# The last unit of a four-layer graph network: two passes over half the query tiles each, against one pass over ten tiles and two late ones over three

## The chip, the core and the metric

The kernel runs on one core of a Trainium2 chip. A core has a matrix engine (TensorE, PE in the profile; PEld is its loading of weights, the stationary operand), a vector engine (VectorE, DVE), an engine for activation functions (ScalarE, ACT), a general one (GpSimd, POOL) and SyncE (SP), which issues transfers. They run side by side and wait for one another by semaphores; 16 DMA engines move data. On chip there is SBUF, where operands lie in 128 partitions, and PSUM, where matmuls accumulate, in eight banks of 512 float32 columns. The metric is the device time of one execution, in microseconds (us); several executions are made and their median counts.

## The reference, cut to what matters

Four layers act on 3327 nodes with 512 features; each ends in `x = layernorm(x + layer(x))`. Layers 0, 2 and 3 are graph attention, layer 1 averages neighbours. The change lies in layer 3, which has 4 heads of 128 features:

```python
h = (x @ W).reshape(N, 4, 128).transpose(1, 0, 2)
si, sj = einsum('hnd,d->hn', h, a1), einsum('hnd,d->hn', h, a2)
e = si[:, :, None] + sj[:, None, :]
e = where(e > 0, e, 0.2 * e)
e = where(adj[None] > 0, e, -9e15)
attn = softmax(e, axis=-1)
out = elu(einsum('hij,hjd->hid', attn, h))
x = layernorm(x + out)
```

## The kernel before, in words

The nodes are 26 tiles of 128 (`NT`); a half of the query nodes is 13 tiles, 1664 columns (`HALF`, `IW`). Layer 3 runs as eight units: for each half of the queries, one unit per head (`s` = 0 to 3). A unit (`unit`, line 429) goes over the 26 key tiles `j`. For each tile, `weights` makes with one VectorE instruction (L420) the unnormalized weights `t` in float32, keys in partitions and queries in columns: a maximum of a row of query terms (`rb`) with a key's term, times the 0/1 mask. ScalarE makes from `t` a step function `y` in 8 bits (L425), from which the softmax denominators come. TensorE multiplies the values of the key tile (`vj`, 128 features as stationary operand, loaded from the DRAM tensor `vd` by SyncE, two tiles at a time) with `t` and accumulates into four PSUM banks `po`, cut as `CUTS` says: 448, 448, 384 and 384 columns (L482). Every four tiles `den` adds up the denominators in the banks `pd` (L446). A product of float32 operands runs as two passes on TensorE, each with its own weight load.

There are three buffers for `t` (pool `at_t`), seven for `y`, three for `vj`. Jobs of the unit before are handed on in a list (`background`) and one is run after each tile; a second list (`aside`) holds other work. So while unit (1, 2) is over and unit (1, 3) runs, its results are transposed (L519), divided by the denominators, put through ELU and added to the residual `g` (`final`, L1472 to L1477), after its denominators went through DRAM and came back as `pes` (L571, L583, L593), and 13 statistics of the first 384 features are taken (L1436). The first two tiles' weights of the next unit are made at the end of a unit (`start`). The order on TensorE is the order of the program; the other engines' instructions are ordered by a planner, except where `tc.keep_in_program_order` pins them among themselves.

The last unit (`last_unit`, line 639) differs. Its 13 query tiles are done in two passes (`e`) over all 26 key tiles: the first over 896 columns (`WA`, 7 query tiles), the second over 768 (`WB`, 6 query tiles). Each pass makes its own weights and steps (L420, L425 with widths 896 and 768), loads the values anew (L677), multiplies them in two banks (L681), and adds denominators in `pd` and in two spare banks (L664), which are copied and summed in the end (L670, L701, L737). The 7 tiles of the first pass are finished while the second pass runs, by jobs (`last_jobs` and `slots`): transposes (L729), reciprocals (L741 to L743), division (L1506), exponential, addition, statistics, the inverse square root on POOL (`rsqrt`, L152 and L153), factors (L1482), scaling by VectorE or ScalarE (L1490, L1488), and a store per tile, issued in turn by SyncE and POOL (L133). The 6 tiles of the second pass are finished after it, in the tail.

Of the kernel before, what the change touches and what calls it, by code (L numbers as in the profile page):

```python
# [1 line left out]

# [5 lines left out]
F32 = mybir.dt.float32  # L8
# [10 lines left out]
P = 128  # L19
# [13 lines left out]
def kernel(  # L33
# [24 lines left out]
    assert WA // 2 <= 512  # L58
    PIECES = (0, 48, 72, 32)
# [40 lines left out]
    c1a = const.tile([P, 2, 4], F32, name="c1a")  # L100
# [5 lines left out]
    nc.vector.tensor_reduce(c1a, c1.rearrange("p o (k s) -> p o s k", s=4), AX.X, ALU.add)  # L106
# [133 lines left out]
    class Layer:  # L240
# [177 lines left out]
        def weights(self, tp, yp, j, h, rb, i0, lo=0, w=IW, pinned=False):  # L418
            t = tp.tile([P, IW], F32, name="t")
            ins = nc.vector.scalar_tensor_tensor(t[:, :w], rb[:, lo:lo + w], self.qc[:, j, h:h + 1],  # L420
                                                 mask_at[0](j, i0 + lo, w), op0=ALU.max, op1=ALU.mult)
            if pinned:
                tc.keep_in_program_order(ins)
            y = yp.tile([P, IW], F8, name="y")
            nc.scalar.activation(y[:, :w], t[:, :w], AF.Sigmoid, bias=self.bi[:, j, h:h + 1],  # L425
                                 scale=self.sc[:, j, h:h + 1], saturate=False)
            return t, y

        def unit(self, pools, half, s, background, aside, final=None, ending=None, following=None):
# [65 lines left out]
            def start(j):  # L495
                if following:
                    self.started[j] = self.weights(tp, yp, j, following[1], self.first_rows[0], following[0] * IW, 0,
                                                   WA if following == (1, NS - 1) else IW, True)
# [140 lines left out]
        def last_unit(self, pools, background, aside, slots):  # L639
            tp, yp, vp, rp, sp, po_p = pools  # L640
            s = NS - 1
            rb = self.first_rows[0]
            started, self.started = self.started, {}
            po = [po_p.tile([P, 512], F32, name=f"po{c}") for c in range(4)]
            pd, seen = self.pd, self.seen
            ob = sp.tile([P, IW], F32, name="ob", bufs=1)
            o = PIECES[s] - 8 * s
            db = sp.tile([P, WA], F32, name="db", bufs=1)
            SPARE = NT // 4 * 4 - 4
            for e, (lo, w) in enumerate(((0, WA), (WA, WB))):  # L650
                wc, nq = w // 2, w // P

                x0 = 64 * (1 - e)
                spare = po[2 - 2 * e:4 - 2 * e]

                def den(j0, ys):
                    for c in range(2):
                        for j, y in enumerate(ys):
                            if j < 2 or len(ys) == 2:
                                a, kk = pd[c], 2 * e + j % 2  # L660
                                assert (kk, c) in seen
                            else:
                                a, kk = spare[c], 2 * (1 - e) + j % 2
                            nc.tensor.matmul(a[32 * kk:32 * kk + 32, :wc], self.sden[:, j0 + j, o:o + 32],  # L664
                                             y[:, c * wc:(c + 1) * wc], start=a is not pd[c] and j0 == 0,
                                             stop=j0 + j >= NT - 2 if a is pd[c] else j0 == SPARE - 4,
                                             skip_group_check=True)
                    if j0 == SPARE - 4:
                        for c in range(2):
                            (nc.scalar.copy if c else nc.vector.tensor_copy)(  # L670
                                db[x0:x0 + 64, c * wc:(c + 1) * wc], spare[c][x0:x0 + 64, :wc])

                late = []
                for j in range(NT):
                    if j % 2 == 0:
                        vj = vp.tile([P, 2, P], F32, name="vj")
                        nc.sync.dma_start(out=vj, in_=self.vd[j * P:(j + 2) * P, s * P:(s + 1) * P]  # L677
                                          .rearrange("(t p) f -> p t f", p=P))
                    t, y = started.pop(j) if not e and j in started else self.weights(tp, yp, j, s, rb, IW, lo, w)
                    for c in range(2):  # L680
                        nc.tensor.matmul(po[2 * e + c][:, :wc], vj[:, j % 2, :], t[:, c * wc:(c + 1) * wc],  # L681
                                         start=j == 0, stop=j == NT - 1)
                    late.append(y)
                    if j % 4 == 0 and j > 0:
                        ys, late = late[:4], late[4:]
                        if j <= SPARE:
                            den(j - 4, ys)
                        else:
                            den(j - 4, ys[:2])
                            den(j - 2, ys[2:])  # L690
                    if background:
                        background.pop(0)()
                    if aside:
                        aside.pop(0)()
                den(NT - 2, late)

                for c in range(2):
                    (nc.scalar.copy if c or not e else nc.vector.tensor_copy)(
                        ob[:, lo + c * wc:lo + (c + 1) * wc], po[2 * e + c][:, :wc])
                for c in range(2):  # L700
                    (nc.scalar.copy if c else nc.vector.tensor_copy)(  # L701
                        db[64 * e:64 * e + 64, c * wc:(c + 1) * wc], pd[c][64 * e:64 * e + 64, :wc])
                jobs = self.last_jobs(e, ob, db, po[2 * e], slots)
                if e == 0:
                    while background:
                        background.pop(0)()
                    while aside:
                        aside.pop(0)()
                    background.extend(jobs)
            return jobs  # L710

        def last_jobs(self, e, ob, db, pe, slots):
            s = NS - 1
            nq = (WB if e else WA) // P
            r_, rc = (a[:, HALF + e * NA:HALF + e * NA + nq, s] for a in (rec, self.rc))
            held = []
            quads = [(q, min(4, e * NA + nq - q)) for q in range(e * NA, e * NA + nq, 4)]  # L720
            takes = []

            def transposed(k):
                if k >= len(quads):
                    return
                q0, n = quads[k]
# [3 lines left out]
                takes.append(slots(q0, n, pt, e))  # L730

            def sums():
# [3 lines left out]
                for q in range(nq):  # L736
                    nc.tensor.matmul(a[:, q, :, :], db[:, q * P:(q + 1) * P], c1a, start=True, stop=True)  # L737
# [998 lines left out]
```

## Time and profile before

| What | us |
|---|---|
| Median of three runs (3217.54 to 3222.51) | 3221.54 |
| Profiled execution, its own time | 3213.32 |
| Its span, first to last instruction | 3211.6 |
| Last unit's first product (L681) starts | 3098.9 |
| First pass's last product group ends, second pass begins | about 3149.5 |
| Last matmul group of denominators starts (L664) | 3190.99 |

The busy times that the prediction shows are sums over instructions in a stretch; an engine that is less busy than the stretch is long was waiting. A timeline row gives start, length, engine, source line, operation, output and inputs, shape, and how many instructions were merged (x4); in brackets the idle time before and what ended it. Starts of equal instructions in a row give their pitch, which is shorter than their length where they overlap. Transfers queued by SyncE stand as SPq.

### The profile page before, as it was taken

The numbers are of one execution on the slowest core, as the hardware profiler recorded it, in microseconds if no ns is written. First come the engines' busy times: TensorE is split into PE (matmuls) and PEld (weight loads), VectorE is DVE, ScalarE is ACT, GpSimd is POOL, SyncE is SP. The second block draws the span as 40 slices with busy tenths as digits, with TensorE's granted clock in tenths as the row PEclk, the third lists the DMA queues.
The fourth block names the chain that finished last, engine by engine and source line by source line (L and its number), as shares of the span: only waits on it lengthen the run. The fifth ranks groups of instructions, "written<-read, shape, count | busy, mean of one in ns | idle before, by whom it ended". The sixth has DMA issues, their size and how long they took to land. (4 is left out here: it accounts for less than half of the span.)

```text
span 3211.6 us, 45012 instructions
## 1 busy us (share of the span) xinstructions
PE 3130.1 (97%) x17934; PEld 1597.4 (50%) x17934; DVE 2611.3 (81%) x2236; ACT 2185.5 (68%) x1759; POOL 308.2 (10%) x500
## 2 busy tenths in 40 slices
PE   8899999999999999999999999999999999999997
PEld 7644343333334467777744333333337655555544
DVE  6799999999986655555489999999999666678887
ACT  2398888899882222232288989899896655568886
POOL 3100000000011122222220000000002000011211
PEclk9999999999999999999999999999999999999998
DMA  9651114111124345556341111111027311123212
GB/s 386 249 168 62 42 52 143 54 43 42 27 84 141 100 124 138 132 138 162 102 141 53 42 36 26 36 42 42 25 84 245 117 42 44 43 54 97 88 43 69
DMA packets 359920, 301.79 MB, mean 94 GB/s; under 512 B 232692, under 2 KB 291902, under 8 KB 358175
## 3 DMA queue, kind: packets, MB, share of 16 engines
q1 hardware_dynamic: 331743, 199.06, 21.1%
q0 software_dynamic: 24656, 96.63, 9.7%
q10 hardware_dynamic: 3312, 3.23, 0.4%
q8 instruction: 142, 2.33, 0.3%
q14 instruction: 67, 0.55, 0.1%
HBM read 221.97 MB, written 76.84 MB: 93 GB/s over the span
## 5 line engine op out<-in xcount | busy, mean ns | idle before, releaser
L846 ACT ACTIVATE y<-t,bi,sc 128x3328 fp8e4<-128x3328 f32 (+1 forms) x520 | 1336.1, 2604 | 97.1 <-PE pd L823 49.3
L867 PE MATMUL po<-t,vj 128*64 128x448 f32 (+1 forms) x6656 | 1269.7, 522 | 12.0 <-DVE t L845 9.4
L867 PEld LDWEIGHTS po<-t,vj 128*64 128x64 f32 x6656 | 458.1, 137 | 686.1 <-issue 625.7
L482 PE MATMUL po<-t,vj 128*128 128x448 f32 (+1 forms) x1456 | 522.6, 516 | 0.6 <-DVE t L420 0.6
L420 DVE SCALAR_TENSOR_TENSOR t<-rba,qc,mk 128x1664 f32<-128x1664 f32 (+2 forms) x234 | 408.5, 1753 | 125.3 <-PE po L482 88.0
L425 ACT ACTIVATE y<-t,bi,sc 128x1664 fp8e4<-128x1664 f32 (+2 forms) x234 | 375.4, 1618 | 189.8 <-DVE t L420 181.8
L482 PEld LDWEIGHTS po<-t,vj 128*128 128x128 f32 x1456 | 272.1, 190 | 235.2 <-issue 148.5
L845 DVE SCALAR_TENSOR_TENSOR t<-rbb,qc,mask 128x3328 f32<-128x3328 f32 (+1 forms) x130 | 380.0, 2985 | 8.4 <-PE po L867 5.4
L845 DVE SCALAR_TENSOR_TENSOR t<-rba,qc,mask 128x3328 f32<-128x3328 f32 (+1 forms) x130 | 380.7, 2982 | 7.0 <-PE po L867 6.2
L845 DVE SCALAR_TENSOR_TENSOR t<-rbb,qc,mk 128x3328 f32<-128x3328 f32 (+1 forms) x130 | 379.3, 2982 | 7.1 <-PE po L867 5.0
L845 DVE SCALAR_TENSOR_TENSOR t<-rba,qc,mk 128x3328 f32<-128x3328 f32 (+1 forms) x130 | 379.7, 2985 | 5.8 <-PE po L867 3.5
L1307 PE MATMUL acc<-zs,kt 128*128 128x512 f32 x1352 | 360.2, 420 | 0.0
L285 PE MATMUL pw<-wsb,xT 128*128 128x264 f32 (+1 forms) x1248 | 297.6, 393 | 14.3 <-DVE vt L295 8.0
L1165 ACT CAST pk<-cy 128x512 f32<-128x512 bf16 x169 | 99.7, 590 | 286.7 <-DVE kt L1179 280.1
L1307 PEld LDWEIGHTS acc<-zs,kt 128*128 128x128 f32 x1352 | 255.6, 189 | 52.1 <-PE pk L1158 0.8
L823 PE MATMUL pd<-y,sden 128*32 128x384 fp8e4 (+1 forms) x3328 | 270.1, 343 | 0.0
L285 PEld LDWEIGHTS pw<-wsb,xT 128*128 128x128 f32 x1248 | 238.5, 194 | 56.5 <-issue 9.8
L1179 DVE SCALAR_TENSOR_TENSOR kt<-pk,mb 128x512 fp32r<-128x512 f32 x169 | 116.0, 687 | 106.7 <-PE pk L1176 106.5
L823 PEld LDWEIGHTS <-sden 128*32 128x32 bf16 x3328 | 88.9, 95 | 165.0 <-issue 149.5
L295 DVE TENSOR_TENSOR vt<-pw,dc 128x256 f32<-128x256 f32 x130 | 49.9, 417 | 79.4 <-ACT dc L286 77.2
L1205 PE MATMUL pz<-wn,xT 128*128 128x512 f32 x208 | 96.9, 610 | 5.4 <-DMA wn<-in_wnT_dram 3.5
L289 ACT COPY rc<-pw 128x8 f32<-128x8 f32 (+1 forms) x78 | 12.8, 164 | 122.1 <-PE pw L285 122.1
(246 smaller groups left out, 2210.6 us busy)
## 6 DMA issues: line engine op xcount, KB each, us to landing
raw<-in_adjT_dram SPq DMA_DIRECT2D x75, 416.0 KB
vj<-v SPq DMA_DIRECT2D x169, 128.0 KB
cy<-ctd POOLq DMA_DIRECT2D x78, 256.0 KB, 4.4
h<-hd SPq DMA_DIRECT2D x61, 256.0 KB
v<-vt SPq DMA_DIRECT2D x50, 256.0 KB
md<-mask SPq DMA_DIRECT2D x26, 416.0 KB
mb<-md SPq DMA_DIRECT2D x169, 64.0 KB
mk<-md SPq DMA_DIRECT2D x50, 208.0 KB
```

The source lines that it names most:

```text
L285: nc.tensor.matmul(pw[e][:, :FW + H], xT[:, c, :], wsb[:, c, e, :], start=c == 0, stop=c == FC - 1)
L420: ins = nc.vector.scalar_tensor_tensor(t[:, :w], rb[:, lo:lo + w], self.qc[:, j, h:h + 1], mask_at[0](j, i0 + lo, w), op0=ALU.max, op1=ALU ...
L425: nc.scalar.activation(y[:, :w], t[:, :w], AF.Sigmoid, bias=self.bi[:, j, h:h + 1], scale=self.sc[:, j, h:h + 1], saturate=False)
L482: nc.tensor.matmul(po[c][k * D:(k + 1) * D, :z - a_], vj[:, j % 2, k * D:(k + 1) * D], ts[k][:, a_:z], start=j == 0, stop=j == NT - 1)
L823: nc.tensor.matmul(pd[c][32 * kk:32 * kk + 32, :w_], lhsT, rhs, start=(kk, c) not in seen, stop=last and j == NT - 1)
L845: nc.vector.scalar_tensor_tensor(to, ro, self.qc[:, j, h:h + 1], m, op0=ALU.max, op1=ALU.mult)
L846: nc.scalar.activation(yo, to, AF.Sigmoid, bias=self.bi[:, j, h:h + 1], scale=self.sc[:, j, h:h + 1], saturate=False)
L867: nc.tensor.matmul(po[c][k * D:(k + 1) * D, :z - a_], vj[:, j % 2, x_:x_ + D], t[:, k, a_:z], start=j == 0, stop=j == NT - 1)
L1165: nc.scalar.copy(pks[k % 2], carry[b, t // 4 * 4][:, t % 4:t % 4 + 2, :])
L1179: nc.vector.scalar_tensor_tensor(kt, pk, NEIGHBOURS, mb[:, t:t + 2, :], op0=ALU.is_le, op1=ALU.mult)
L1205: nc.tensor.matmul(pz, xT[:, c, :], wn[:, c, :], start=c == 0, stop=c == FC - 1)
L1307: nc.tensor.matmul(acc, kts[b, t][:, s * P:(s + 1) * P], zs(t, c), start=t == 0 and c == 0, stop=t == NT - 1 and c == 1)
```

## The change

The weights of a key tile are now made for all 1664 columns in one pass, by two instructions on VectorE and two on ScalarE: 1280 columns (ten query tiles, `KEPT`) into the buffer `t`, and 384 columns (three query tiles) into the first bytes of the key tile's own mask, whose first half is of no more use (`kept`). The pass multiplies only the first three cuts, 1280 columns, into three banks, and adds all denominators into `pd`. Afterwards the three remaining query tiles are multiplied from the kept weights: a pass over two tiles (256 columns, bank `po[3]`) and one over the last (128 columns, bank `po[0]`). Their values are loaded ahead: four tiles into `vj` buffers, the others by two transfers into two `t` buffers. While these late passes run, the ten tiles are finished by jobs set between the products (quads A, B, C of 4, 4 and 2 tiles; D is the two tiles of the first late pass, E the last tile), with the order on VectorE and ScalarE pinned. Stores are all issued by SyncE. One exponential on a single column stands ahead of the others (`warm`). `start` makes the two first tiles with the new widths. The finishing loop that stood after `L3.attention` is gone.

```diff
+    KEPT = CUTS[3][0]
...
-        def weights(self, tp, yp, j, h, rb, i0, lo=0, w=IW, pinned=False):
+        def weights(self, tp, yp, j, h, rb, i0, pinned=False, cuts=((0, IW, None),)):
...
+            for lo, hi, kept in cuts:
+                o = t[:, lo:hi] if kept is None else kept
+                ins = nc.vector.scalar_tensor_tensor(o, rb[:, lo:hi], self.qc[:, j, h:h + 1],
+                                                     mask_at[0](j, i0 + lo, hi - lo), op0=ALU.max, op1=ALU.mult)
...
+                nc.scalar.activation(y[:, lo:hi], o, AF.Sigmoid, bias=self.bi[:, j, h:h + 1],
+                                     scale=self.sc[:, j, h:h + 1], saturate=False)
...
+        def kept(self, j):
+            return mask_tiles.tiles[j][:, :4 * (IW - KEPT)].bitcast(F32)
+
+        def last_weights(self, tp, yp, j, rb, pinned=False):
+            return self.weights(tp, yp, j, NS - 1, rb, IW, pinned, ((0, KEPT, None), (KEPT, IW, self.kept(j))))
...
-            for e, (lo, w) in enumerate(((0, WA), (WA, WB))):
...
+            def den(j0, ys):
+                for c in range(2):
+                    for j, y in enumerate(ys):
+                        for e, (a_, w_) in enumerate(((c * (WA // 2), WA // 2), (WA + c * (WB // 2), WB // 2))):
+                            kk = 2 * e + j
+                            nc.tensor.matmul(pd[c][32 * kk:32 * kk + 32, :w_], self.sden[:, j0 + j, o:o + 32],
+                                             y[:, a_:a_ + w_], start=False, stop=j0 == NT - 2, skip_group_check=True)
...
+            for j in range(NT):
+                if j % 2 == 0:
+                    vj = values(j)
+                t, y = started.pop(j) if j in started else self.last_weights(tp, yp, j, rb)
+                for c, (a_, z) in enumerate(CUTS[:3]):
+                    nc.tensor.matmul(po[c][:, :z - a_], vj[:, j % 2, :], t[:, a_:z], start=j == 0, stop=j == NT - 1)
...
+            for e, (lo, w) in enumerate(((0, WA // 2), (0, WB // 2))):
                 for c in range(2):
+                    keep((nc.vector.tensor_copy, nc.scalar.copy)[c](
+                        db[64 * e:64 * e + 64, c * w:(c + 1) * w], pd[c][64 * e:64 * e + 64, :w]))
+            for c, (a_, z) in enumerate(CUTS[:3]):
+                keep((nc.vector.tensor_copy if c == 1 else nc.scalar.copy)(ob[:, a_:z], po[c][:, :z - a_]))
...
+            f = slots(transposed)
+            near = {j: values(j) for j in range(0, 4, 2)}
+            far = []
+            for lo in (4, 4 + HALF):
+                n = min(HALF, NT - lo)
+                v = tp.tile([P, IW], F32, name="t").rearrange("p (t f) -> p t f", f=P)
+                nc.sync.dma_start(out=v[:, :n, :], in_=self.vd[lo * P:(lo + n) * P, s * P:(s + 1) * P]
+                                  .rearrange("(t p) f -> p t f", p=P))
...
+            def product(acc, j, lo, hi):
+                nc.tensor.matmul(acc[:, :hi - lo], near[j // 2 * 2][:, j % 2, :] if j < 4 else far[j - 4],
+                                 self.kept(j)[:, lo - KEPT:hi - KEPT], start=j == 0, stop=j == NT - 1)
...
+            jobs = [nothing] * 3 + [
+                lambda: sums(*A, qp.tile([P, 512], F32, name="pl", tag="q")), lambda: [reciprocals(*A), f.turn(*A)],
+                lambda: [f.divide(*A), sums(*RB, po[1])], lambda: sums(*RC, po[2]),
+                lambda: [reciprocals(*RB), reciprocals(*RC)], nothing, lambda: f.turn(*B), lambda: f.divide(*B), lambda: f.turn(*C),
+                lambda: f.divide(*C), lambda: [f.add(*A), f.stats(*A)], lambda: f.add(*B), lambda: f.factors(*A), lambda: f.stats(*B),
+                lambda: f.ones(*A), lambda: f.add(*C)]
+            for j in range(NT):
+                product(po[3], j, KEPT, cut)
+                if jobs:
+                    jobs.pop(0)()
...
+            out_of(po[3], KEPT, cut)
+            jobs = [nothing] * 5 + [lambda: f.stats(*C), lambda: f.factors(*B), nothing, nothing, lambda: f.turn(*D), lambda: f.divide(*D),
+                                    lambda: [f.ones(*B), f.factors(*C), f.add(*D), f.stats(*D), f.ones(*C, (8, 9))]]
+            for j in range(NT):
+                product(po[0], j, cut, IW)
+                if jobs:
+                    jobs.pop(0)()
...
+            out_of(po[0], cut, IW)
+            f.turn(*E)
+            f.divide(*E)
+            f.factors(*D)
+            f.ones(*D)
+            f.add(*E)
+            f.stats(*E)
+            f.factors(*E)
+            f.ones(*E, (HALF - 1,))
...
+                    def divide(q0, n):
...
+                        keep(nc.vector.tensor_tensor(h[q0][:, :n], pts[q0][:, :n],
+                                                     rec[:, HALF + q0:HALF + q0 + n, NS - 1:NS]
+                                                     .to_broadcast([P, n, P]), op=ALU.mult))
+                        ex[q0] = fp.tile([P, 4, P], F32, name="e", tag="xr" if third_ else "e")
+                        keep(nc.scalar.activation(ex[q0][:, :n], h[q0][:, :n], AF.Exp))
...
+                    def stats(q0, n):
+                        for q in range(q0, q0 + n):
+                            keep(nc.vector.bn_stats(out=st[:, q, 1, :], in_=g[:, q, FB:]))
+                            keep(nc.vector.bn_aggr(out=mv[:, q, :], in_=st[:, q, :, :]))
+                        rsqrt(rs[:, q0:q0 + n, 0], mv[:, q0:q0 + n, 1])
...
+                    def ones(q0, n, by_dve=()):
+                        for q in range(q0, q0 + n):
+                            y = g[:, q, :]
+                            if q in by_dve:
+                                keep(nc.vector.tensor_scalar(y, y, rs[:, q, 0:1], rs[:, q, 1:2], op0=ALU.mult, op1=ALU.add))
+                            else:
+                                keep(nc.scalar.activation(y, y, AF.Identity, bias=rs[:, q, 1:2], scale=rs[:, q, 0:1]))
+                            store_tile(out, y, HALF + q, nc.sync)
...
+                    keep(nc.scalar.activation(warm, valid, AF.Exp))
```

## The prediction

> **What bounds the kernel now.** First the page: TensorE (PE) is busy nearly everywhere, so time is gained only where it waits or where it has stopped. The last unit starts at 3098.9 us, so next come the busy times by stage: two passes, then the tail.
>
> ```profile
> PE 3130.1 (97%) x17934; PEld 1597.4 (50%) x17934; DVE 2611.3 (81%) x2236; ACT 2185.5 (68%) x1759; POOL 308.2 (10%) x500
> ...
> 3098.90:3150.00 51.10, 46.98 (x174) 21.31 (x171) 45.03 (x63) 38.14 (x40) 9.24 (x16) 1.00 0.16 39
> 3150.00:3191.10 41.10, 40.55 (x175) 21.94 (x176) 32.38 (x56) 29.97 (x34) 4.24 (x5) 1.00 0.25 81
> 3191.10:3211.60 20.50, 2.44 (x22) 2.03 (x19) 8.60 (x27) 5.39 (x8) 4.30 (x7) 0.60 0.22 77
> ```
>
> Columns are length, busy PE, PEld, DVE, ACT, POOL, granted clock. VectorE (DVE) is nearly as full as PE in the first pass; in the tail PE is idle. The timelines give pitches:
>
> ```profile
> 3097.04 1.14 DVE L420 SCALAR_TENSOR_TENSOR t<-rba,qc,mk 128x896 f32<-128x896 f32 x1
> 3104.16 4.34 DVE L420 SCALAR_TENSOR_TENSOR t<-rba,qc,mk 128x896 f32<-128x896 f32 x4
> 3144.86 3.03 DVE L420 SCALAR_TENSOR_TENSOR t<-rba,qc,mk 128x896 f32<-128x896 f32 x3
> ...
> 3140.97 0.19 PEld L681 LDWEIGHTS po<-t,vj 128*128 128x128 f32 x1 [0.19 <-issue]
> 3141.35 0.19 PEld L681 LDWEIGHTS po<-t,vj 128*128 128x128 f32 x1 [0.19 <-issue]
> ...
> 3192.03 1.42 PEld L737 LDWEIGHTS po<-c1a,db 128*128 128x128 f32 x12
> ```
>
> A 448-column matmul pass repeats every 0.3755 us (two passes per fp32 product). The last weights of the first pass are made by 3145.95. The tail, from PE's last product to the stores:
>
> ```profile
> 3190.99 0.50 PE L664 MATMUL pd<-y,sden 128*32 128x384 fp8e4 x4
> ...
> 3200.68 2.22 ACT L1488 ACTIVATE g<-g,rs 128x512 f32<-128x512 f32 x3 [4.81 <-DVE rs L1482]
> ...
> 3202.02 0.61 DVE L1490 TENSOR_SCALAR g<-g,rs 128x512 f32<-128x512 f32 x1
> ...
> 3203.19 0.54 POOL L133 DMA_DIRECT2D out_dram<-g  x1 [0.15 <-issue]
> ...
> GB/s 0 0 0 0 0 0 0 0 0 0 0 0 0 0 0 0 111 386 381 347 304 265 270 366 400 309 386 174 0 0 0 0 0 0 0 0 0 0 0 19
> ```
>
> PE is done at 3191.5, compute at 3202.6, 11.1 us later: six query tiles are finished behind it. The last line is the DMA view of 3195 to 3212 in 40 slices: six stores queue up and drain until 3206.9, 4.3 us after compute; 4.7 us more follow to 3211.6.
>
> **The change, part by part.** *Weights.* The trace has 896 columns at 1.142 us and 768 at 1.008: 1.05 ns a column; 896 repeats at (4.34-1.14)/3 = 1.067, a fixed 0.12. So 1280 takes 1.46, 384 takes 0.52, the pair 1.98, against about 1.06 + 0.93 before in two passes: DVE's sum stays, but all of it now stands ahead of the late products. ScalarE (ACT) likewise keeps its two sigmoids per tile (about 1.44 + 0.69 = 2.13 us, 55 in all).
>
> *The unit before it.* Weights of tile 0 are longer by 0.9 us, in a gap where DVE waits 3.06 us for PE: free, and 0.9 if that cover were gone. Tile 1 runs on from 3097.04.
>
> *Main pass, ten query tiles.* PE: 26 x 2 x (0.3755 x 2 + 0.3225) = 55.8; denominators about 1.07 per four tiles with the switch, 7.0; transposes of unit 2, 1.6: 64.4, so not before 3163.3. DVE from 3097.04: 25 pairs, 49.5; unit 2's leftovers by their pitch 16.5 (transposes 2.5, reductions 0.9, sums 0.9, three elementwise steps 6.0, 13 statistics 6.2): 3163.0. ACT: 55 + four table loads of 1.28 and the exponentials, 62.5, also just below. Three engines within 3%: they stall each other through three t buffers. The same sum for the old first pass gives 3140.6 (with 0.6 for a copy) against 3145.95, so 5.3 us of DVE waits; 2.9 were waits for PE and are smaller where a pair lasts 1.98 against PE's 2.15. I take 2.0: DVE ends at 3165.0, PE's last product with its denominators at 3167.2. Ends: 3165.2 without waits, 3170.5 with all 5.3.
>
> *Late passes.* At N/1.2 + 2.5 ns, which fits both widths in the trace, 256 columns take 0.216 and 128 take 0.110 a pass: 26 x 2 of each, 11.2 + 5.7. Total product time is the old one, only later. Sums, 26 matmuls at 0.112 (the L737 row: (1.42-0.19)/11), 2.9; transposes 1.4; switches 0.8: 22.0 us, PE ends at 3189.2. Beside it DVE finishes ten tiles: from its turn after quad C's division, 10.3 us in, adds, statistics (0.405 a tile), factors and two scalings take 12.7 with small waits for rsqrt, so it is free at 23.0, 1.0 behind PE. Engine order is pinned here, so anything late delays all behind it on DVE.
>
> The 128-column price needs the weight load (0.19 us each) to hide behind a 0.110 pass; loads alone repeat at 0.112, and behind 448 columns no time is left for one, so 0.11 is nearest. Ends: 0.11 and 0.216 if load and pass add up, 5.5 us. [...]
>
> *Values ahead.* Two loads of 13 and 9 tiles go into the t slots of tiles 23 and 24, free about 6.0 and 3.8 us before the main pass ends. SyncE issued four DMAs of as many rows in 4.86 us, 1.2 each; a row of 512 bytes takes 26 ns of one of 16 engines:
>
> ```profile
> 2851.48 4.86 SPq L536 DMA_DIRECT2D hd<-ob  x4
> ...
> q1 hardware_dynamic: 272, 0.13, 14.7%
> ```
>
> (14.7% of 16 engines over 3 us, by 272 packets.) So 1664 rows need 2.7 us at best, 5.9 at the pace of one small load, plus 1 to start and 0.5 to land: 4.2 to 7.4 after issue, at worst 1.4 us after the main pass. First use is 4 x 0.43 = 1.7 us after it. Nothing, or up to 2; I take 0.5. Nothing waits behind them on SyncE until the first stores.
>
> *Tail and stores.* After 23.0 one tile is left: copy 0.27, transpose 0.4, division 0.4, exponential 0.35, adds 0.7, statistics 0.5, rsqrt 0.9, factor and scaling 0.75: 27.2 after the main pass, at 3194.4 against 3202.6. Only three tiles' stores fall near the end, so the queue is drained about 2.5 us after compute, not 4.3. SyncE alone issues 13 tiles' stores at 0.35 to 0.45 each, spread over 11 us; without that spread it would be 5 us. The early Exp on one column moves a table load of 1.28 under copies: nothing, as the old load also lay under PE's sums.
>
> Sum: 3167.2 + 0.5 + 27.2 + 2.5 + 4.7 = 3202.1, against 3211.6: 9.5 us less. The profiled execution took 3213.3, 8.2 under the median of the three runs, whose spread is 5.0; taken off the median 3221.5, this gives 3212.0. Bounds: the best ends (3165.2, no late values, DVE 1 us quicker) give -13; the worst without a rival (3170.5, 2 late) -5.
>
> **The rivals.** *The three engines of the main pass hold each other up more.* For it: the sums of unit 2 waited for a DMA (1.9 us), and reductions now come about 2.7 us later, as three longer tiles stand ahead. Against: PE has up to two finished tiles in hand. All 5.3 plus 2.7 put the main pass's end at 3173 or so: -3.7, 3217.8, the same. Chance 15%.
>
> *Weight loads do not hide at 128 columns.* For: no row of that width. Against: the 448 row. 5.5 more on PE less 1.0 that DVE is behind: -5.0, 3216.5, the same. Chance 8%.
>
> *Slower: the values are not ahead.* Mechanism: the t slot is given back only when the main pass's end is reached, so the first load is issued then, or its 512-byte rows crawl. For: one load of 1.66 MB in 1-KB rows took 8.7 us from POOL. Against: slots are reused tile by tile, and vj loads were issued as soon as PE left their slot. Each us past 1.7 costs one; alone it decides against the change from a landing 11.7 us after the main pass. But PE idles meanwhile, and the tail shows a granted clock of 0.60 after idling: at 0.60 the first late pass takes 7.5 us more, and then a landing at 4.2 decides; one at 12 gives +8, 3230. [...] Chance 9%, with other ways of being slower.
>
> **How the numbers follow.** The forecast has 68%, its own range 3208 to 3217. A measurement of this kernel tells about 0.2%, 6.4 us, from no change; 5% of the forecast's lie inside that. Faster 0.63, same 0.28, slower 0.09. From 3206, the best end and the spread of the runs, to 3219, which takes in the two mild rivals, 8 in 10 are held.
>
> **What would show it.** One pass of some 68 us with 52 L420-like pairs and DVE over 90% busy; late passes of 22 us with the clock at 1.00 and PE without a gap at tile 4; weight loads at 0.11 in the last 5.7 us; compute ending about 5 us after PE's last product, not 11; stores drained 2.5 us later. A main pass beyond 3171, a gap at the first late products, a clock below 1.00 there, or DVE still adding when PE has long ended would make it wrong.

## The result, and the profile after

The changed kernel takes 3210.2 us in the median (3206.3 to 3217.6, 13 runs) against 3218.8 for the kernel before (3213.4 to 3222.8, 13 runs): a ratio of 0.9979, with a 95% interval of 0.9970 to 0.9987. That is 8.6 us less by the medians, 7.0 by the means, and between 4 and 10 by the interval. The prediction was 3212.0, between 3206 and 3219.

The two profiled executions can't be set against each other as wholes: the one of the changed kernel took 3217.6 us, the one of before 3213.3, but in the former layer 3's first product starts 11.5 us later, though the layers up to there are computed in the same way. So everything below is measured from the start of unit (1, 2), the unit ahead of the last. From there to the end of the span it is 193.8 us before and 186.3 after, 7.5 less.

First the busy line of the page after the change, which answers to the one of before (PE 97%):

```profile
PE 3139.9 (98%) x17986; PEld 1609.5 (50%) x17986; DVE 2609.8 (81%) x2240; ACT 2186.7 (68%) x1763; POOL 308.3 (10%) x499
```

Then the busy times by stage: unit (1, 2); the main pass, from its first product to the first late product; from there to the end of compute; and the end. Columns as in the prediction.

```profile
3029.39:3111.89 82.50, 81.47 (x325) 42.59 (x325) 81.61 (x98) 70.35 (x54) 14.83 (x25) 1.00 0.19 51
3111.89:3182.95 71.06, 67.49 (x273) 33.26 (x273) 54.73 (x62) 62.09 (x63) 9.48 (x17) 0.98 0.17 44
3182.95:3210.15 27.20, 22.07 (x147) 20.00 (x143) 18.09 (x63) 12.98 (x21) 6.44 (x10) 0.95 0.36 128
3210.15:3215.70 5.55, 0.00 (x0) 0.00 (x0) 0.03 (x1) 0.00 (x0) 0.00 (x0) 0.50 0.16 49
```

What the reader is to see: in unit (1, 2) VectorE is full (81.6 of 82.5; before it was 70.0 of 81.0). In the main pass it is not (54.7 of 71.1), ScalarE is busier (62.1), and the granted clock is 0.98. In the third stage TensorE goes on to work for 22 of 27 us, where before the last six tiles were finished beside an idle TensorE. Rows of the timeline show the rest, engine by engine: the first and the last of the kept weights on VectorE, the issue of the two big transfers of values and the first products that use them, the second late pass on TensorE and the last transpose, the weight loads of that pass, the last scaling, and the stores in SyncE's queue:

```profile
3027.65 1.15 DVE L424 SCALAR_TENSOR_TENSOR mk<-rba,qc,mk 128x384 f32<-128x384 f32 x2 [0.68 <-DMA rba<-r]
...
3108.56 2.74 DVE L424 SCALAR_TENSOR_TENSOR mk<-rba,qc,mk 128x384 f32<-128x384 f32 x5
...
3113.20 0.63 DVE L424 SCALAR_TENSOR_TENSOR mk<-rba,qc,mk 128x384 f32<-128x384 f32 x1
...
3177.62 2.14 SPq L717 DMA_DIRECT2D t<-v  x2
...
3185.59 0.68 PE L722 MATMUL po<-mk,t 128*128 128x256 f32 x2
...
3201.42 3.74 PE L722 MATMUL po<-mk,t 128*128 128x128 f32 x32
3206.14 0.33 PE L708 MATMUL pt<-ident,ob 128*128 128x128 f32 x1 [0.99 <-DVE ob L749]
3201.31 3.65 PEld L722 LDWEIGHTS po<-mk,t 128*128 128x128 f32 x32
3209.63 0.55 DVE L1543 TENSOR_SCALAR g<-g,rs 128x512 f32<-128x512 f32 x1
3199.23 9.74 SPq L134 DMA_DIRECT2D out_dram<-g  x12
3210.20 0.83 SPq L132 DMA_DIRECT2D out_dram<-g  x2
```

And the DMA view of 3195 to 3216, in 40 slices:

```profile
GB/s 16 0 0 0 0 0 0 0 0 109 375 363 379 371 378 24 0 51 382 359 359 371 375 390 379 332 289 355 351 4 117 289 90 0 0 0 0 0 0 0
```

The tile `mk` is a key tile's mask, into whose first bytes the 384 kept weights go. There are 26 instructions for them. The planner put two just ahead of unit (1, 2) and 23 into it, and only the last starts in the main pass: they need no `t` buffer, so nothing held them back once their row of query terms (`rba`) had arrived. The matmuls of 128 columns start every 0.11 us. Transfers end at about 3212.2, 2.0 us after compute.

By the prediction's own terms, in us:

| Term | predicted | trace after |
|---|---|---|
| Unit (1, 2), against before | 0 | +1.4 |
| Main pass to first late product | 68.3 | 71.1 |
| Values late | 0.5 | 0 |
| First late product to the end of compute | 27.2 | 27.2 |
| Last stores and the end | 7.2 | 5.5 |
| From the last unit's first product to the end (before: 112.7) | 103.2 | 103.8 |
| All, against before | -9.5 | -7.5 |

Two terms cost more than predicted and two less. The chain of work that ended last shows where the main pass is held (start, length, engine, tile, line; `...` stands for pieces left out):

```profile
3121.01 8.70 POOL pes L593 x15
3129.72 1.92 DMA pes<-dd
...
3144.64 1.28 ACT L1501
3145.93 0.63 ACT e L1501
3146.58 1.28 ACT L428
3147.88 1.58 ACT y L428 x2
...
3149.83 2.04 ACT y L428 x2
3151.89 1.28 ACT L1501
...
3153.51 1.28 ACT L428
3154.83 1.34 issue
3156.17 2.64 ACT y L428 x3
...
3159.18 10.48 PE po L683 x24
```

Up to 3158.9 the chain in the main pass doesn't run over TensorE at all. It begins with the denominators of head 2: POOL issues their small transfers one after the other, 15 of them in 8.70 us, and they are back at 3131.6, so head 2's finishing starts only some 20 us into the pass. Then the chain runs over VectorE and ScalarE. L1501 is the exponential of that finishing, and each of the four stands between two table loads of 1.28 us, one for itself and one to go back to the sigmoid of L428. At the end of it TensorE waits, and then runs slowly. Its timeline:

```profile
3151.38 4.56 PE L683 MATMUL po<-t,vj 128*128 128x448 f32 x12 [0.50 <-DVE t L424]
3155.87 0.79 PE L674 MATMUL pd<-y,sden 128*32 128x448 fp8e4 x10
3158.26 0.92 PE L674 MATMUL pd<-y,sden 128*32 128x448 fp8e4 x6 [1.59 <-ACT y L428]
3159.11 6.26 PE L683 MATMUL po<-t,vj 128*128 128x448 f32 x12
```

And the busy times of two stretches of 3.4 us, in and behind that wait:

```profile
3156.30:3159.70 3.40, 1.75 (x14) 0.61 (x10) 3.01 (x2) 3.40 (x4) 0.00 (x0) 1.00 0.00 0
3159.73:3163.14 3.41, 3.41 (x7) 1.56 (x6) 1.61 (x2) 3.41 (x5) 0.00 (x0) 0.50 0.00 0
```

TensorE waits 1.59 us for a step function; the clock is 0.50 for the next 3.41 us, which costs half of it, 1.7: twelve matmuls, six products of two passes each, take 6.26 us and not 4.56.

### The profile page after: what moved, and what is told of

Its sections match the earlier page's. It is cut to its first block, busy times and chain, and to the rows that moved or that the text cites. A ratio compares the mean times of both kernels' runs of the same rounds, so it can differ in the third digit from the quotient of the medians.

```text
span 3215.7 us, 45079 instructions
## 1 busy us (share of the span) xinstructions
PE 3139.9 (98%) x17986; PEld 1609.5 (50%) x17986; DVE 2609.8 (81%) x2240; ACT 2186.7 (68%) x1763; POOL 308.3 (10%) x499
## 3 DMA queue, kind: packets, MB, share of 16 engines
q8 instruction: 142, 2.33, 0.3%
## 5 line engine op out<-in xcount | busy, mean ns | idle before, releaser
L424 DVE SCALAR_TENSOR_TENSOR t<-rba,qc,mk 128x1664 f32<-128x1664 f32 (+1 forms) x208 | 393.4, 1897 | 120.9 <-PE po L491 81.1
L428 ACT ACTIVATE y<-t,bi,sc 128x1664 fp8e4<-128x1664 f32 (+1 forms) x208 | 358.5, 1733 | 180.4 <-DVE t L424 173.4
L170 ACT ACTIVATE h<-h,rs 128x512 f32<-128x512 f32 x65 | 49.5, 808 | 71.1 <-DVE rs L167 71.1
```

What stands on the lines that cost most here:

```text
L424: ins = nc.vector.scalar_tensor_tensor(o, rb[:, lo:hi], self.qc[:, j, h:h + 1], mask_at[0](j, i0 + lo, hi - lo), op0=ALU.max, op1=ALU.mult)
L428: nc.scalar.activation(y[:, lo:hi], o, AF.Sigmoid, bias=self.bi[:, j, h:h + 1], scale=self.sc[:, j, h:h + 1], saturate=False)
```

## The experiments

The theory to test: ScalarE's eight table loads in the main pass, which lie in a bunch, make TensorE wait and set the length of the pass (A). The first rival: the kept weights made ahead upset unit (1, 2) and the start of the pass (B). The second, from the prediction: VectorE and three `t` buffers hold the engines up. All lengths are taken as in the table above; the expectations of the first runs count the main pass from 0.4 us earlier, and so name 71.5 for 71.1.

**All weights pinned.**

```diff
-                t, y = started.pop(j) if j in started else self.last_weights(tp, yp, j, rb)
+                t, y = started.pop(j) if j in started else self.last_weights(tp, yp, j, rb, True)
```

> All VectorE weight instructions of the last unit, the 1280 columns and the 384 kept ones, are pinned in the order of the program, so the 26 kept weights can no longer be made ahead while unit (1, 2) runs. After the change they were made there (VectorE 81.2 us busy of 82.1), and the main pass, first product to first late product, took 71.5 us where the prediction had 68.3. Theory A, ScalarE sets the main pass (two sigmoids per tile at a pitch of 1.945 us and eight table loads of 1.28 us): unit (1, 2) goes back to 81.0, VectorE in the main pass rises from 55.2 to some 65 us busy, and the main pass stays at 71 to 72. Theory B, the instructions made ahead are what upset the pass: it comes to 68.3, as the prediction's sum had it. Third way, three t buffers and a pair of 1.98 us on VectorE hold the engines up as the first rival had it: 73 or more.

Unit (1, 2) took 81.1, the main pass 94.7. The busy times of the pass:

```profile
3102.18:3196.92 94.74, 75.75 (x277) 36.50 (x273) 65.72 (x85) 62.77 (x63) 9.48 (x17) 0.87 0.13 33
```

And waits in the timelines of VectorE and TensorE:

```profile
3120.94 0.27 DVE L603 TENSOR_TENSOR pes<-pes 128x104 f32<-128x104 f32 x1 [5.21 <-DMA pes<-dd]
3127.97 0.69 DVE L1498 TENSOR_TENSOR h<-pt,rec 128x512 f32<-128x512 f32 x1 [4.11 <-PE pt L529]
3123.38 4.11 PE L683 MATMUL po<-t,vj 128*128 128x448 f32 x6 [4.17 <-DVE t L424]
```

The number lies with the third way, but no engine is full. Pinning both kinds of weights gave another order: on VectorE the first sums and the first division stand ahead of weights that TensorE needs sooner. The sums wait 5.2 us for a transfer, and the weights behind them wait too; TensorE waits 4.2 us for those weights, and its transposes come behind their products; so the division waits 4.1 us for the transposes, and the next weights stand behind the division. So this run says what a bad order costs (23.7 us, the mean clock of 0.87 among it), and nothing on A or B. The question was put again in another way.

**Kept weights not ahead, the rest free.** Only the 384-column instructions are pinned, and so come behind the two first tiles of the last unit.

```diff
-                if pinned:
+                if pinned or kept is not None:
                     tc.keep_in_program_order(ins)
```

> As after the change, but only the 26 kept weights (384 columns) are pinned on VectorE, behind the two first tiles of the last unit: they can't be made ahead in unit (1, 2), and the planner is free to place all the rest, unlike in the run with every weight pinned, where the first divisions stood ahead of weights that TensorE needed first and the main pass took 94.8 us. Eight table loads, as after. VectorE then has 26 x 0.53 = 13.8 us more in the main pass than after (55.4 busy), some 69 us. If the instructions made ahead are what makes the pass possible at all: the main pass is set by VectorE, 73 us or more against 71.1. If ScalarE's table loads alone set it: 71 to 72. If making ahead upsets it: 68.3 as the prediction's sum. Unit (1, 2) goes from 82.5 back to 81.1.

Unit (1, 2) 81.1, main pass 68.9, and 182.8 us in all against 186.3. VectorE now has 64.2 us of work in the pass, and yet the pass is shorter, as its busy times show:

```profile
3105.21:3174.14 68.93, 65.82 (x277) 32.55 (x273) 64.18 (x85) 62.49 (x63) 9.45 (x17) 1.00 0.18 45
```

So the weights made ahead are not needed, and they cost: 1.4 us in unit (1, 2), and a wait of 1.4 us at the pass's third tile, where VectorE comes late out of its full unit. Here TensorE waits 0.39 and 1.39 us for weights and 1.24 for a step function, 0.5 less in sum than after, and the clock stays at 1.00. B holds for its part, 1.4 and some 0.5 us; that the clock stayed up is not shown to be its work, as two runs further down have the waits of after and a clock of 1.00, with a main pass of 69.4. That the pass can't do without the weights ahead (73 us or more) falls, and so does the second rival as what sets the length: VectorE has 9.5 us more to do here, and the pass isn't longer.

**No table loads.** The ELU of head 2 is left out by this.

```diff
-                    nc.scalar.activation(e[:, :n], h[:, :n], AF.Exp)
+                    nc.scalar.activation(e[:, :n], h[:, :n], AF.Sigmoid)
```

> The exponential of ELU in the finishing of head 2 is a sigmoid, for both halves of the queries; so no table is loaded for it in the main pass: eight table loads of 1.28 us (10.3 us of ScalarE) go, the rest of the work stays. The ELU of head 2 is left out by it. Theory A (ScalarE sets the main pass): it shortens by 3 us or more, from 71.5 to 66 to 68, where VectorE and TensorE (64.4 us of it) bind. Theory B (the kept weights made ahead, or the waits among three t buffers, set it): within 0.7 us of 71.5. Unit (1, 2) holds four exponentials no more either where head 1 is finished in the same way only if the same line serves it; its length says so: 82.1 if not.

**Exponentials in pairs.** Same computation: `final` keeps two quads, takes their exponentials one behind the other, then adds.

```diff
...
+                    held.append((h, y, n))
+                    if len(held) < 2 and q0 + n < HALF:
+                        return
+                    es = []
+                    for h_, y_, n_ in held:
+                        e = fp.tile([P, 4, P], F32, name="e")
+                        nc.scalar.activation(e[:, :n_], h_[:, :n_], AF.Exp)
+                        es.append(e)
...
```

> The exponentials of head 2's finishing are taken in pairs, two quads at a time, so that ScalarE's order has six table loads in place of eight; nothing is left out. Theory A: ScalarE is let off 2.6 us, and the main pass falls from 71.5 to between 68.9 and 70.5 (less than 2.6 where VectorE has to wait for the second quad's exponential). Theory B: 71.5 within 0.7.

The busy times of the main pass without table loads:

```profile
3100.32:3166.53 66.21, 64.82 (x273) 32.66 (x273) 54.11 (x62) 51.81 (x55) 9.45 (x17) 1.00 0.18 48
```

And with six of them in place of eight:

```profile
3102.13:3168.54 66.41, 65.02 (x274) 32.67 (x274) 54.18 (x62) 59.06 (x61) 9.46 (x17) 1.00 0.18 47
```

Busy ScalarE falls from 62.1 to 51.8 and 59.1 us. Against 71.1, all eight gone give 4.9 us, and two gone already give 4.7. But 1.7 of that is the slow clock, which the two runs with a main pass of 69.4 didn't have behind the same waits. Against those, eight loads less (10.3 us of ScalarE) give 3.1 and two less (2.6 us) give 2.9; the 68.9 to 70.5 expected of the pairs started from a pass with the slow clock in it. So A holds, but not as a sum of ScalarE's work. What goes, with two loads as with eight, are the waits of 0.50 and 1.59 us and what is lost around them; TensorE's waits in both runs are only those at the start (0.62 for a copy, counted in the unit before, and 1.39 for weights).

**One round less, at two places.** The exponential of one quad becomes a sigmoid, and two loads go with it; the ELU of those tiles is left out.

```diff
-                    nc.scalar.activation(e[:, :n], h[:, :n], AF.Exp)
+                    nc.scalar.activation(e[:, :n], h[:, :n], AF.Sigmoid if n == 1 else AF.Exp)
```

> As after the change, but the last exponential of head 2's finishing (the quad of one tile, 128 columns, 0.31 us, with two table loads around it, 2.87 us together) is a sigmoid, so its two loads go: the ELU of that one tile is left out, in both halves of the queries. After the change ScalarE did this round at 3151.9 to 3154.8, TensorE then waited 0.5 us for weights and 1.6 us for a step function of ScalarE's at 3158.3, and the granted clock was 0.57 in the next 4 us. If this round and the slow clock behind it are what the main pass loses: 66.2 to 67, from 71.1. If only the sum of ScalarE's work counts: 71.1 less 2.6 to 2.9, about 68.3. If neither: 71.

```diff
-                    nc.scalar.activation(e[:, :n], h[:, :n], AF.Exp)
+                    nc.scalar.activation(e[:, :n], h[:, :n], AF.Sigmoid if q0 == 0 else AF.Exp)
```

> As after the change, but the first exponential of head 2's finishing (a quad of four tiles, 0.63 us and two table loads) is a sigmoid instead, so the same two loads go from another place: the ELU of those four tiles is left out, in both halves of the queries. The last round stays. If the place of the last round decides, TensorE still waits behind it: 70 to 71. If the sum of ScalarE's work counts, wherever it lies before the wait: as without the last round, between 66.2 and 68.3.

Without the last round 67.0 us, with the wait of 0.5 for weights left; without the first 67.6, and TensorE's timeline has a wait of 0.63 at the place of the 1.59:

```profile
3155.78 0.92 PE L674 MATMUL pd<-y,sden 128*32 128x448 fp8e4 x6 [0.63 <-ACT y L428]
```

So it matters little which round goes: ScalarE falls behind over all four, and any 2.6 us given back ahead of the wait take most of it away. The clock stays at 1.00 in both runs; against the 69.4 of a pass with that clock they are worth 2.4 and 1.8 us.

**Not ahead, and in pairs.** Both edits of above together.

> Both edits: kept weights pinned behind the first two tiles (not made ahead), and the exponentials of head 2's finishing paired; nothing is left out. Paired alone gave a main pass of 66.4 and a unit (1, 2) of 82.5 us. If VectorE has the room (69 us of work against 66): unit (1, 2) 81.1 and main pass 68 to 70, so from the start of unit (1, 2) to the end 182 to 184 us against 181.6; if the weights made ahead are needed, 73 or more in the main pass and 187 or more in all.

Unit (1, 2) 81.1, main pass 67.7, 181.5 us in all: the same as pairs alone (181.6). What is won in unit (1, 2) is given back in the pass, where VectorE (64.1 us busy of 67.7) makes TensorE wait three times, 2.2 us together.

**Some ahead, and in pairs.** Kept weights of tiles 2 to 13 are free, those from 14 on pinned.

```diff
-                if pinned:
+                if pinned or kept is not None and j >= 14:
                     tc.keep_in_program_order(ins)
```

> As the run with paired exponentials, but only the kept weights of tiles 2 to 13 may be made ahead, those from 14 on are pinned on VectorE behind the first two tiles of the last unit; nothing is left out, and there are six table loads. With all made ahead, unit (1, 2) took 82.5 us and TensorE waited 2.0 us at the first tiles of the main pass (66.4 us in all); with none, 81.1 and 67.7. If it is VectorE being full in unit (1, 2) that costs there and at the start: 81.1 and 65.5 to 66.7, so 179.6 to 181 us from the start of unit (1, 2) to the end, less than either (181.6, 181.5). If the two can't be had together: 181.3 or more.

The busy times of unit (1, 2) and the main pass:

```profile
3020.69:3102.47 81.78, 81.39 (x327) 42.67 (x325) 77.34 (x87) 70.76 (x57) 14.79 (x25) 1.00 0.20 54
3102.47:3167.43 64.96, 64.90 (x277) 32.74 (x274) 58.38 (x73) 59.36 (x61) 9.45 (x17) 1.00 0.19 47
```

TensorE is busy for 64.90 of 64.96 us: in the main pass it waits for nothing any more. In all 179.4 us. The same kernel timed:

> The same kernel as the last run with some weights made ahead and paired exponentials, timed. From the start of unit (1, 2) to the end it took 179.4 us, the kernel before 193.8 and the changed kernel 186.3. So 14.4 us less than before, a ratio of 0.9955, and 6.9 us less than after the change (0.9979). If the layers before, which differ by some us from execution to execution, hide it: above 0.998.

3203.3 us in the median (3197.5 to 3206.7, 6 runs) against 3217.5 for the kernel before (11 runs), a ratio of 0.9953 (0.9939 to 0.9967). This version beats both kernels; its profile gives 179.3 us from unit (1, 2) on, 14.5 less than before and 7.0 less than after the change.

**Stores by two queues again.**

```diff
-                            store_tile(out, y, HALF + q, nc.sync)
+                            store_tile(out, y, HALF + q, (nc.sync, nc.gpsimd)[q % 2])
```

> The stores of the last unit are issued in turn by SyncE and GpSimd, as before the change; all else is as after it. After the change the last transfer ended 2.0 us after compute and the span 3.5 us after that, 5.5 in all, where the kernel before had 4.3 and 4.7, 9.0 in all. If the queue of GpSimd is what made the old end long (its transfers last, and its end notified later): 6.7 to 9 us from the end of compute to the span's end. If it was only the six tiles stored at once: 5.5 within 0.5. Main pass and late passes as after, 71.5 and 22.2.

Main pass and late passes as after (71.0 and 22.2). From the first late product to the end of compute 28.2 us in place of 27.2, and 6.5 to the end in place of 5.5, a little below the 6.7 to 9 expected if GpSimd's queue makes the end long. The stores cost 1.0 us at each of two places. The first was in nobody's sum: POOL computes the inverse square roots, and in its timeline a store that it issues stands between the two instructions (L153, L154) of one:

```profile
3198.82 0.29 POOL L153 TENSOR_SCALAR rs<-mv 128x4 f32<-128x4 f32 x1 [1.93 <-DVE mv L1531]
3199.34 0.64 POOL L134 DMA_DIRECT2D out_dram<-g  x1 [0.22 <-ACT g L1545]
3200.01 1.06 POOL L154 TENSOR_TENSOR rs<-rs,power 128x4 f32<-128x4 f32 x1
```

**Values not ahead.** `near` and the two transfers are gone; `product` calls `values(j)` for every second tile.

```diff
...
-                nc.tensor.matmul(acc[:, :hi - lo], near[j // 2 * 2][:, j % 2, :] if j < 4 else far[j - 4],
+                if j % 2 == 0:
+                    near[0] = values(j)
+                nc.tensor.matmul(acc[:, :hi - lo], near[0][:, j % 2, :],
```

> As after the change, but the values of the late passes are not loaded ahead in two big transfers; they come two tiles at a time through the three vj buffers, once for each late pass. After the change TensorE had no gap in the late passes (22.2 us, 27.2 to the end of compute). If the values ahead are what allows it: with some 2.7 us from issue to landing and three buffers, a pair of tiles comes every (2.7 + 0.86) / 3 = 1.2 us in the first late pass and every 1.05 in the second, against products of 0.86 and 0.44; the sums and transposes between the products of the first pass hide most of its share, the second grows from 5.7 to some 13, so the late passes take 28 to 32 and compute ends 33 to 37 after the first late product. If three buffers keep up: within 1 of 22.2 and 27.2. Main pass 71.1 as after.

The late passes take 39.5 us and compute ends 44.1 after their start: 16.9 more, and worse than either number expected. SyncE's queue shows why, and TensorE's timeline and its busy time from 3199.65 on what it did:

```profile
3194.85 1.96 SPq L134 DMA_DIRECT2D out_dram<-g  x4
3196.91 10.78 SPq L665 DMA_DIRECT2D vj<-v  x9
3207.78 3.77 SPq L134 DMA_DIRECT2D out_dram<-g  x6
3211.65 1.88 SPq L665 DMA_DIRECT2D vj<-v  x3
3200.32 2.93 PE L716 MATMUL po<-mk,vj 128*128 128x128 f32 x12 [2.78 <-DMA vj<-v]
3214.71 2.93 PE L716 MATMUL po<-mk,vj 128*128 128x128 f32 x12 [3.69 <-DMA vj<-v]
...
3199.65:3217.64 17.99, 12.60 (x50) 11.11 (x50) 3.08 (x10) 3.24 (x5) 1.27 (x2) 0.50 0.52 168
```

The loads stand behind stores on SyncE, which wait for scaled tiles; the last three were issued after six stores and TensorE waited 3.7 us for them. The stores are not the whole of it. The first late pass, with no store yet ahead of its loads, already takes some 18.6 us (its products end at about 3196.7), where after the change it is 15.3 (3182.95 to 3198.28), as TensorE waits for loads there too. And from 3199.65 on the granted clock is 0.50: at 1.00 the 12.60 us of TensorE's work there would be some 6.3 less, an estimate from these two numbers. In this run the main pass, unchanged, took 69.4 us, not 71.1: the wait of 1.59 us is there, but the clock stays at 1.00 behind it.

**One late pass.** 384 columns at once, and three tiles finished together; the two calls for the last tile go.

```diff
-            D, E = (KEPT // P, HALF - KEPT // P - 1), (HALF - 1, 1)
-            cut = KEPT + D[1] * P
+            D, cut = (KEPT // P, HALF - KEPT // P), IW
...
```

> As after the change, but the three late tiles are multiplied in one pass of 384 columns, and finished together. Product time is the same (26 x 2 x 0.3225 = 16.8 us), so with sums and transposes the pass is some 21.5 to 22. If the cut in two and one pays by leaving one tile behind the last product: three tiles then take 29 to 31 us from the first late product to the end of compute, against 27.2, and their three stores end together, 5.5 to 6.5 to the span's end against 5.5. If VectorE sets the end either way: 27 to 28 and 5.5.

From the first late product to the end of compute 29.1 us, and 5.0 to the end: 34.1 against 32.7. The cut in two and one is worth 1.4 us. The main pass took 69.35 us, as in the run before, with the same waits and the clock at 1.00.

## Why the prediction was right, and where it wasn't

*The tail.* "27.2 after the main pass" was measured as 27.2, and the late passes of 22.0 as 22.2. TensorE had no gap at tile 4, waited 0.99 us for VectorE before the last transpose (the prediction had VectorE 1.0 behind), and compute ended 5.0 us behind the last product (about 5 were predicted; before it was 11.1). From the last unit's first product to TensorE's last one it is 93.3 us and was 92.6, so the gain lies behind that: 6.1 us of compute, and 3.5 at the stores. Leaving three tiles for the end and then one is where it comes from; with three at once 1.4 us of it are lost.

*The 128-column price.* 32 weight loads of the second late pass start over 3.65 - 0.19 us, so every 0.112 us, and the products with them, though a load alone takes 0.19 us. Products (3.74 us from 3201.42 on) and loads (3.65 us from 3201.31 on) run side by side. The load hides; the dearer end (5.5 us) and its rival are out.

*Values ahead.* Half a microsecond was put in, none was needed: both transfers were issued from 3177.6 on, before the first late product (3182.95), and the first of their values are used at 3185.6, behind eight sums that TensorE does in between. The other side is larger than the run on it expected: with the values two tiles at a time it is 16.9 us more, twice the whole gain. There the slow clock in the late passes, which the prediction had in its rival, did come (0.50 from 3199.65 on).

*Stores and end.* 7.2 were predicted and 5.5 measured. The drain was mis-sized by little (2.5 against 2.0); the 4.7 us that followed it before became 3.5, where the prediction had kept them. With POOL's queue back in use they are 1.0 longer, and the scaling is 1.0 later besides.

*The unit before.* "Free" was the step that failed by its mechanism: it looked at tile 0's longer weights alone. The kept weights have a place of their own to go to, so nothing holds them back, and the planner put 25 of the 26 into unit (1, 2) or just ahead of it. That fills VectorE and costs 1.4 us there, which the run without them ahead gave back (81.1).

*The main pass.* Mis-sized, 68.3 against 71.1, and for another reason than the prediction thought. It had VectorE over 90% busy; it was at 77%, since 25 instructions had gone ahead. Its sum for ScalarE came out right (62.5, measured 62.1) by two errors that cancel: a tile's two sigmoids repeat every 1.94 us and not 2.13, and there are eight table loads and not four. And a sum "just below" was no cover: the four rounds lie in 21 us of the pass (3133.9 to 3154.8), where ScalarE falls behind. In pairs, with two loads less, the pass is 2.9 us shorter at the same clock (66.41 us against 69.35 with one late pass). The parts, by the runs: 64.9 of work on TensorE (predicted 64.4); waits of 1.42 at the start, which go when fewer weights are made ahead; 0.50 and 1.59 behind the exponentials, which go with two table loads; 0.8 in the denominators around that wait (10 and 6 matmuls in 0.79 and 0.92 us, where 16 in a row take 0.94); and 1.7 of slow clock. Their sum is 70.9, against 71.1 measured.

*The rivals.* Three engines holding each other up came true in kind, but not in size: 4.4 us of waits (69.36 less 64.96) against the forecast's 3.9, and 1.7 of clock, where the rival had 9.7. The values coming late did not happen. The clock, which the prediction feared in the late passes, dropped in the main pass instead, behind a wait of 1.59 us, where in the first pass before the change one of 2.33 us had left it at 1.00 (its row stands in the last section).

The sum of -9.5 against the trace's -7.5 is the 2.8 of the main pass and the 1.4 of the unit before, less 1.7 at the stores and 0.5 for the values. So that the total came within 2.0 us is in part luck: 4.2 us that the sum didn't have stand against 2.2 that it had too much. Without the slow clock the trace would have -9.2; two of the four profiled runs with that same wait had it and two had not. The timing, -8.6 by the medians and -7.0 by the means, can't tell the two apart. How many of the 13 timed runs had it stays open, as only one of them has a trace.

## What to carry to other kernels

When work gets a buffer of its own, ask what now no longer holds it back: an instruction without a scarce buffer is free to be made far ahead, and it may fill an engine where that is not wanted (VectorE was busy for 81.6 of 82.5 us in unit (1, 2), and that cost 1.4). Count table loads by switches, not by functions (here eight of 1.28 us for four exponentials), and put exponentials side by side: two loads less, 2.6 us of ScalarE, were worth 2.9 us here, and eight less, 10.3 us, only 3.1. What they cost was not their own time, but the wait of 1.59 us that they caused at TensorE, what was lost around it, and in two traces of four a clock of 0.50 behind it (1.7 us). A queue that issues stores which wait for compute must not hold loads that the same compute needs (TensorE waited 3.7 us for three loads behind six stores), and an engine with short steps on the path should issue no stores (POOL's made compute end 1.0 us later).

## What the runs showed of the hardware that was not expected

The granted clock was 0.50 for one stretch of 3.41 us after a wait of 1.59 us, in two executions (after the change, and with two store queues; main passes of 71.06 and 71.04 us); in two others (values not ahead, one late pass; 69.36 and 69.35) the same wait, with the same work around it, was followed by 1.00. The clock's records change only at multiples of 3.41 us. In the first two the wait lay whole in one such stretch (3156.31 to 3159.73 after the change), and TensorE was busy for 1.77 and 1.76 us of it, with L683's products for 0.62 and 0.69 and with denominators for the rest. With one late pass the wait lay across two stretches. With the values not ahead it lay whole in one as well (3151.87 to 3155.28), near its end; TensorE was busy for 1.82 us, with L683's products for 0.91. So TensorE was at work for half of the stretch behind which the clock fell. The busy times with the slow clock and without it hardly differ, while those of the products do. Before the change a wait was longer and the clock stayed:

```profile
3128.46 1.77 PE L681 MATMUL po<-t,vj 128*128 128x448 f32 x4 [2.33 <-DVE t L420]
...
3127.01:3130.43 3.42, 1.77 (x4) 0.68 (x4) 3.42 (x8) 2.89 (x5) 0.00 (x0) 1.00 0.02 5
3130.43:3133.84 3.41, 2.25 (x13) 0.85 (x13) 3.41 (x6) 2.37 (x3) 0.00 (x0) 1.00 0.14 41
```

That wait lies across two stretches. In its second one TensorE is busy for 1.77 us too, all of it with L681's products, and the next stretch has 1.00. That the products hold the clock up and the narrow 8-bit denominators do less would fit these numbers; it is the author's guess from them, and no run tried it.

A table load of 1.28 us held ScalarE for no longer than itself: the exponential behind the one at 3144.64 starts at 3145.93, and behind none of the eight in the main pass after the change do more than 0.02 us pass before the next instruction.
